# Four graph layers on one core: mask pieces pinned to unit steps, mask sums spread over the units, carries copied a step ahead, and first work of the next stage issued while sums end

## The chip, the cores and the metric

The kernel runs on one core of one Trainium2 chip. The metric is the device time of one execution in microseconds. A core has five engines with a queue each: PE (matrix products), DVE (vector operations), ACT (activations and copies), POOL and SP (here mostly queues that issue DMAs, as ACT's queue does too).

## What is computed

A feature matrix `x` (3327 x 512) goes through four graph layers over one 0/1 adjacency matrix `adj` (3327 x 3327, int32). Each layer's output is added to its input and normalised by row:

```
def attention_layer(x, adj, W, a, heads):       # layers 0, 2, 3 (8, 8 and 4 heads)
    Wh = x @ W                                  # per head
    e = leaky_relu(Wh @ a1 [:, None] + Wh @ a2 [None, :], 0.2)
    p = softmax(where(adj > 0, e, -9e15), axis=neighbours)
    return p @ Wh                               # layers 2 and 3: elu of it

def sage_layer(X, A):                           # layer 1
    keep = (A > 0) & (cumsum(A > 0, axis=1) <= 64)
    mean = (keep @ X) / max(keep.sum(1), 1)
    xj = leaky_relu(mean @ W_nb.T + b_nb);  xi = leaky_relu(X @ W_line.T + b_line)
    return xi + where(keep.sum(1) > 0, xj, 0)

x = layernorm(x + layer(x))                     # four times
```

## The kernel before

The 3327 nodes are 26 tiles of 128 rows; 13 tiles are a half (1664 nodes). Everything of size 3327 x 3327 is made on the fly: one byte mask of the adjacency (`mask`, neighbours on the partitions) is kept on chip for all layers. It is made in layer 0 from the int32 matrix in 104 pieces of 128 x 832: `mask_load` brings one piece (`raw`, 416 KB, issued in turn on SP's and ACT's queues), `mask_set` turns it into bytes, on DVE (L521) or on ACT (L519).

An attention layer is done in three parts.

- Projection. For each tile, `project1` transposes `x` (`pt`, L253; copied to `xT` by ACT, L255), and `project2` multiplies it by the weights (`pw`, L264), makes the exponentials `dc` (L265) and the logit columns `fc`, and writes the scaled features `vt` to DRAM (`v`). `prepare` (L292), for one half, makes the exponential columns `rc` and `qc`, transposes `rc` (`pr`, L304), copies it (`rr`, L306) and stores it (`r`), and makes the scale and bias `sc` and `bi`. `cut` (L316) splits `dc` into bf16 pieces (`pc`) for the softmax denominators and places them in `sden` (L336) and `sm` (L341). `mean` (L279) multiplies the summed `x` by the weights and stores one row `ms`.
- Attention. A loop over two halves of the receiving nodes and four units `s` in each; a unit takes two heads in layers 0 and 2 and one head in layer 3. A unit (`unit`, L345) loads the row factors `rb` of its heads over all partitions and then walks over the 26 tiles of neighbours, one step `j` each. Per step and head DVE makes `t` (L396), ACT makes the byte `y` of its sign (L399), and PE adds the product of `t` with the features `vj` to four sums `po` (L405). Every second step PE adds the denominators of two earlier steps to `pd` (L365, `den`): products of `y` with `sden` in every unit, and products of the mask with `sm`, the mask sums, in unit 0 only. Each step also takes one job from a list `background` and one from a list `aside`. At its end a unit copies `po` to `ob` (L419 on ACT, L421 on DVE); transposes of `ob` (`pt`, L427), copies `hb` and stores to DRAM (`hd`) are jobs of the next unit. After a half's last unit `pd` is copied (`db`) and turned into reciprocals (`pe`, L458, and `rec`).
- Finish. `finish` loads two tiles of the result and of the layer's input (`h`, `xr`), divides, adds, and normalises them (`norm_rows`: Sqrt at L154, the normalising activation at L161). It runs inside the next layer's first part.

In layer 0 the first 38 mask pieces are program text of the projection; the other 66 are `aside` jobs, one a step, each step loading a piece and setting the one before it. The counts of neighbours per block of rows (`count_jobs`, L537) are jobs of units 0 and 2 of the first half, behind empty jobs that hold them back; they give `ctd`, the running counts, in DRAM.

Layer 1 (`sage`, L572) first makes the two linear maps of all tiles (`pz`, L612, and `pi`, L615) and then 13 blocks of 256 receiving nodes. For a block, `kept(b, t)` brings the carry (the running count ahead of the tile, `cy`) into a PSUM bank `pk` (copy by ACT, L680), adds the tile's own running count to it (PE, L681), and compares with 64 on DVE (`kt`, L684). PE then forms the sums `acc` of the kept neighbours (L711) for each of the two tiles of a block in three bf16 parts; `output` finishes the tile, and two jobs (layer 2's `project1` and `project2` of the tile) are taken at steps 11 and 17 of the next sum. Layer 3's projection is `third` (L736), which also finishes layer 2; layer 3's own finish is done in its attention by `later` and `final`.

Two things set the order of the work. On PE the order is that of the program text:

```
ctx.enter_context(tc.manual_schedule(engines={mybir.EngineType.PE}))
```

On DVE, ACT, POOL and SP a scheduler sets the order when the kernel is built, by its own estimate of when each instruction's inputs are ready, so that an instruction may move far from its place in the text. `tc.keep_in_program_order(ins)` takes one instruction out of this freedom: it stays behind the instruction of its engine that is just ahead of it in the text. Pools of buffers give the other ties: `at_t` has 6 buffers for `t` in layers 0 and 2, `at_y` 7 or 8 for `y`, `raw` two for the mask pieces of the attention.

## Time and profile before

| what | value |
|---|---|
| median of the runs | 3514.73 us (3510.88, 3514.73, 3521.66) |
| profiled execution, its own time | 3513.41 us |
| its span | 3511.7 us |
| granted PE clock, mean over the span | 0.981 |
| busy: PE, DVE, ACT, POOL | 95%, 77%, 69%, 5% |
| layer 0: projection; attention | 0 to 164; 164 to 990 us |
| layer 1: linear maps; blocks | 990 to 1205; 1205 to 1840 us |
| layer 2: attention | 1844 to 2640 us |
| layer 3: projection; attention and end | 2640 to 2800; 2800 to 3512 us |

A line of instruction groups in the profile has the source line, engine, operation and tiles, the count, then the busy time in us and the mean in ns of one, and the idle time of the engine ahead of them with what ended most of it. A line of a timeline has start and duration in us, and in brackets the idle time ahead of it with what ended it. PE 95% busy does not mean that PE sets the pace everywhere: it is a mean over stages[...].

### The profile page before, as it was taken

The page shows a single profiled execution, that of the slowest core. Times are in us where ns is not written, and L with a number is a line of the kernel's source. Part 1 is how long each engine was busy: PE and PEld are TensorE (multiplying, and loading weights), DVE is VectorE, ACT ScalarE, POOL GpSimd, SP SyncE. Part 2 cuts the span into 40 slices and gives each one's busy share as a digit, 9 for nine tenths or more (in the row PEclk, how much of TensorE's full clock was granted, in tenths as well). Part 3 has the DMA queues.
Part 4 walks back from the last instruction along what each step waited for, and adds up shares of the span by engine and source line. Part 5 has one row for each costly group of instructions (what it writes and reads, how often), then busy time and mean ns, then how long its engine had stood idle before and what let it go on. Part 6 is the DMA issues. An engine that isn't in the chain of part 4 may idle for free.

```text
span 3511.7 us, 48175 instructions
## 1 busy us (share of the span) xinstructions
PE 3340.7 (95%) x18926; PEld 1705.4 (49%) x18926; DVE 2689.9 (77%) x2751; ACT 2440.2 (69%) x2369; POOL 181.1 (5%) x289
## 2 busy tenths in 40 slices
PE   7899999999989999999989999999998899999997
PEld 6644444444444455545544444444446655455553
DVE  5599999999967544344339999999997666668886
ACT  3678988999953343443328999899996655558885
POOL 1000000000000111111110000000001000000000
PEclk9999999999999999999999999999998999999998
DMA  9713311111133422222211111111106411112211
GB/s 360 231 46 119 99 52 38 56 29 47 37 113 126 133 83 66 75 67 70 70 52 41 48 48 46 52 47 42 38 25 211 149 44 44 44 43 91 81 39 48
DMA packets 208454, 276.67 MB, mean 79 GB/s; under 512 B 19321, under 2 KB 140355, under 8 KB 208228
## 3 DMA queue, kind: packets, MB, share of 16 engines
q1 hardware_dynamic: 173622, 157.37, 14.0%
q0 software_dynamic: 22736, 89.80, 8.1%
q10 hardware_dynamic: 11870, 26.42, 2.3%
q8 instruction: 149, 2.44, 0.3%
q14 instruction: 77, 0.63, 0.1%
HBM read 204.92 MB, written 68.60 MB: 78 GB/s over the span
## 4 chain that ended last, share of the span: by engine, by line
PE 59%; issue 26%; DVE 6%; DMA 5%; ACT 3%; POOL 1%; POOLq 0%; SPq 0%; ACTq 0%; DVEq 0%
PE po L405 33%; PE acc L711 9%; PE pw L264 5%; PE pd L365 4%; DVE t L396 3%; PE pz L612 2%; PE pi L615 2%; DMA raw<-in_adjT_dram 1%; DMA cy<-ctd 1%; ACT y L399 1%; PE pt L427 1%; PE pk L681 1%; DVE kt L684 1%; DMA v<-vt 1%; PE pt L253 1%
## 5 line engine op out<-in xcount | busy, mean ns | idle before, releaser
L396 DVE SCALAR_TENSOR_TENSOR t<-rb,qc,mask 128x1664 f32<-128x1664 f32 x1040 | 1959.5, 1945 | 205.8 <-PE po L405 159.0
L399 ACT ACTIVATE y<-t,bi,sc 128x1664 fp8e4<-128x1664 f32 x1040 | 1772.2, 1766 | 331.9 <-PE pd L365 312.0
L405 PE MATMUL po<-t,vj 128*64 128x448 f32 (+3 forms) x8320 | 1944.2, 521 | 24.1 <-DVE t L396 22.5
L405 PEld LDWEIGHTS po<-t,vj 128*64 128x64 f32 (+1 forms) x8320 | 857.8, 148 | 984.7 <-issue 677.3
L711 PE MATMUL acc<-zs,kt 128*128 128x512 bf16 x1352 | 402.8, 380 | 0.0
L264 PE MATMUL pw<-wsb,xT 128*128 128x264 f32 (+1 forms) x1248 | 303.1, 398 | 21.7 <-DVE vt L270 9.9
L680 ACT CAST pk<-cy 128x256 f32<-128x256 bf16 x338 | 123.9, 374 | 270.5 <-DVE kt L684 218.6
L711 PEld LDWEIGHTS <-kt 128*128 128x128 fp8e4 x2028 | 198.3, 98 | 227.5 <-issue 32.0
L264 PEld LDWEIGHTS pw<-wsb,xT 128*128 128x128 f32 x1248 | 241.3, 198 | 66.6 <-ACT xT L255 13.3
L365 PE MATMUL pd<-y,sden 128*32 128x448 fp8e4 (+1 forms) x4160 | 259.9, 341 | 8.4 <-ACT y L399 8.2
L684 DVE SCALAR_TENSOR_TENSOR kt<-pk,mask 128x256 fp8e4<-128x256 f32 x338 | 140.9, 421 | 158.2 <-PE pk L681 157.6
L711 PE MATMUL acc<-zl,kt 128*128 128x512 bf16 x676 | 256.6, 380 | 0.6 <-DMA zl<-zd 0.6
L365 PEld LDWEIGHTS <-sden 128*32 128x32 bf16 x4160 | 118.0, 96 | 160.3 <-issue 137.7
L270 DVE TENSOR_TENSOR vt<-pw,dc 128x256 f32<-128x256 f32 x156 | 59.0, 417 | 98.7 <-ACT dc L265 86.8
L681 PE MATMUL pk<-mask,upto 128*128 128x256 fp8e4 x338 | 92.2, 273 | 20.4 <-ACT pk L680 19.7
L353 POOL DMA_DIRECT2D rb<-r x40 | 21.4, 537 | 1674.7 <-DVE t L396 1571.8
L612 PE MATMUL pz<-wn,xT 128*128 128x512 f32 x208 | 97.1, 611 | 6.4 <-ACT xT L606 6.4
L268 ACT COPY fc<-pw 128x8 f32<-128x8 f32 (+1 forms) x156 | 22.9, 165 | 106.0 <-PE pw L264 99.2
L521 DVE TENSOR_SCALAR mask<-raw 128x832 fp8e4<-128x832 int32 (+1 forms) x78 | 45.1, 594 | 63.9 <-DMA raw<-in_adjT_dram 63.6
L615 PE MATMUL pi<-wl,xT 128*128 128x512 f32 x208 | 93.5, 592 | 0.0
L585 POOL DMA_DIRECT2D cy<-ctd x91 | 67.8, 745 | 403.6 <-ACT pk L680 270.3
L692 DVE SCALAR_TENSOR_TENSOR y<-acc,cnt,bnb 128x512 f32<-128x512 f32 x26 | 19.5, 751 | 79.0 <-PE acc L711 79.0
(165 smaller groups left out, 1780.3 us busy)
## 6 DMA issues: line engine op xcount, KB each, us to landing
vj<-v SPq DMA_DIRECT2D x312, 128.0 KB
rb<-r POOLq DMA_DIRECT2D x40, 832.0 KB, 4.6
cy<-ctd POOLq DMA_DIRECT2D x78, 256.0 KB, 3.9
v<-vt SPq DMA_DIRECT2D x75, 256.0 KB
h<-hd SPq DMA_DIRECT2D x65, 256.0 KB
raw<-in_adjT_dram ACTq DMA_DIRECT2D x38, 416.0 KB
raw<-in_adjT_dram SPq DMA_DIRECT2D x37, 416.0 KB
hd<-hb SPq DMA_DIRECT2D x60, 256.0 KB
```

The costliest lines, as they stand in the source:

```text
L264: nc.tensor.matmul(pw[e][:, :FW + H], xT[:, c, :], wsb[:, c, e, :], start=c == 0, stop=c == FC - 1)
L365: nc.tensor.matmul(pd[c][32 * kk:32 * kk + 32, :w_], lhsT, rhs, start=(kk, c) not in seen, skip_group_check=final is not None, stop=last a ...
L396: nc.vector.scalar_tensor_tensor(t, rb[k], self.qc[:, j, h:h + 1], mask[:, j, i0:i0 + IW], op0=ALU.max, op1=ALU.mult)
L399: nc.scalar.activation(y, t, AF.Sigmoid, bias=self.bi[:, j, h:h + 1], scale=self.sc[:, j, h:h + 1], saturate=False)
L405: nc.tensor.matmul(po[c][k * D:(k + 1) * D, :z - a_], vj[:, j % 2, k * D:(k + 1) * D], ts[k][:, a_:z], start=j == 0, stop=j == NT - 1)
L585: nc.gpsimd.dma_start(out=cy[:, :n, :], in_=ctd[t:t + n, b * GW:(b + 1) * GW] .rearrange("(o t) i -> o t i", o=1).to_broadcast([P, n, GW]))
L612: nc.tensor.matmul(pz, xT[:, c, :], wn[:, c, :], start=c == 0, stop=c == FC - 1)
L615: nc.tensor.matmul(pi, xT[:, c, :], wl[:, c, :], start=c == 0, stop=c == FC - 1)
L680: nc.scalar.copy(pk, carry[b, t // 4 * 4][:, t % 4, :])
L681: nc.tensor.matmul(pk, upto, mask[:, t, i0:i0 + GW], start=False, stop=True, skip_group_check=True)
L684: nc.vector.scalar_tensor_tensor(kt, pk, NEIGHBOURS, mask[:, t, i0:i0 + GW], op0=ALU.is_le, op1=ALU.mult, saturate=False)
L711: nc.tensor.matmul(acc, kts[t][:, s * P:(s + 1) * P], zs[:, t, c, :] if c < 2 else zl[:, t, :], start=t == 0 and c == 0, stop=t == NT - 1 ...
```

## The change

- Masks. All 104 pieces are one list. The first 60 belong to the projection (three steps of the list at two tiles of five, two at the others), all on DVE; the other 44 are the `aside` jobs of the first two units, and the instruction that sets a piece is pinned to its place in the program text, behind its step's `t` (DVE) or `y` (ACT). The empty jobs ahead of the counts are gone.
- Mask sums. In layers 0 and 2 the mask products of steps `j0` and `j0 + 1` are made in unit `j0 // 2 % 4` instead of all in unit 0.
- Carry. `kept` issues the copy of the next tile's carry into the other `pk` bank right after its own product, instead of its own copy ahead of it.
- Layer 1's last sum. The job at step 17 of the very last sum (layer 2's `project2` of the tile before the last) is left for after the sum.
- `prepare(1)` and `cut(1)`, the parts for the second half of the tiles, become jobs of unit 0 in all three attention layers.
- The pool of `rb` is opened ahead of those of `t`, `y` and `vj`, so that it lies at another place in memory.
- A function `ending` is called in the last unit of layers 0 and 2 ahead of its last `den`: it issues the finish of the layer's first two tiles there, instead of after the attention.

The diff:

```diff
-        def cut(self, pool, half):
+        def cut(self, pool, half, tag="pc", bufs=1):
...
-            pc = pool.tile([P, HALF, H, 8], BF, name="pc")
+            pc = pool.tile([P, HALF, H, 8], BF, name="pc", tag=tag, bufs=bufs)
             nc.gpsimd.memset(pc, 0.0)
-            rest = pool.tile([P, HALF, H], F32, name="rest")
+            rest = pool.tile([P, HALF, H], F32, name="rest", bufs=1)
...
-        def unit(self, pools, half, s, background, aside, final=None):
+        def unit(self, pools, half, s, background, aside, final=None, ending=None):
...
-                if s == 0:
+                if s == (j0 // 2 % NS if HS == 2 else 0):
                     for j, c, k, e in order:
                         a_, w_ = part(c, e)
                         go(c, j0 + j, k, e, self.sm[:, j0 + j, 32 * k:32 * k + 32],
...
+            if ending:
+                ending()
             den(NT - 2, late)
...
-            with tc.tile_pool(name="at_t", bufs=3 * self.HS, reuse_waits="tile") as tp, \
+            with tc.tile_pool(name="at_r", bufs=self.HS + 1, reuse_waits="tile") as rp, \
+                    tc.tile_pool(name="at_t", bufs=3 * self.HS, reuse_waits="tile") as tp, \
                     tc.tile_pool(name="at_y", bufs=4 * self.HS - (self.li == 0), reuse_waits="tile") as yp, \
                     tc.tile_pool(name="at_v", bufs=4, reuse_waits="tile") as vp, \
-                    tc.tile_pool(name="at_r", bufs=self.HS + 1, reuse_waits="tile") as rp, \
...
-                mask_set(held[k - lag], *pieces[k - lag], on_act=(k - lag) in on_act)
+                ins = mask_set(held[k - lag], *pieces[k - lag], on_act=(k - lag) in on_act)
+                if pinned:
+                    tc.keep_in_program_order(ins)
...
+                order = [(b, t) for b in range(len(blocks)) for t in range(NT)]
+                at = [0]
+
+                def carry_in(k):
+                    if k < len(order):
+                        b, t = order[k]
+                        if t % 4 == 0 and groups:
+                            load_carry()
+                        nc.scalar.copy(pks[k % 2], carry[b, t // 4 * 4][:, t % 4, :])
+
                 def kept(b, t):
-                    t0, i0 = blocks[b]
-                    if t % 4 == 0 and groups:
-                        load_carry()
-                    pk = pks[t % 2]
-                    nc.scalar.copy(pk, carry[b, t // 4 * 4][:, t % 4, :])
+                    k = at[0]
+                    at[0] += 1
+                    assert order[k] == (b, t)
+                    i0 = blocks[b][1]
+                    pk = pks[k % 2]
                     nc.tensor.matmul(pk, upto, mask[:, t, i0:i0 + GW], start=False, stop=True,
                                      skip_group_check=True)
+                    carry_in(k + 1)
                     kt = kp.tile([P, GW], F8, name="kt")
...
-                            if jobs and t in (11, 17):
+
+                            if jobs and (t == 11 or t == 17 and not (last and s == G - 1)):
                                 jobs.pop(0)()
...
                 L3.project2(pp, bank, wsb, *pend)
-                L3.prepare(pp, 1)
                 L3.mean(pp, bank, wsb)
-                L3.cut(pp, 1)
...
-                L3.attention(later=later, final=final)
+                L3.attention(lambda pool, half, s: [lambda: L3.prepare(fp, 1, "xr", 2), lambda: L3.cut(fp, 1, "e", 2)]
+                             if (half, s) == (0, 0) else [], later=later, final=final)
...
-            EARLY = 3 * NT // 4
-            msteps = mask_steps(rw0, [(t, q) for t in range(EARLY) for q in range(2)], 3, ())
+            pieces = [(t, q) for t in range(NT) for q in range(2)] + [(t, q) for q in (2, 3) for t in range(NT)]
+            EARLY = 2 * NT + 8
+            msteps = mask_steps(rw0, pieces[:EARLY], 3, (), False)
...
-                for _ in range(2):
+                for _ in range(3 if t % 5 < 2 else 2):
                     if msteps:
                         msteps.pop(0)()
...
-            L0.prepare(pp, 1)
             L0.mean(pp, bank, wsb)
-            L0.cut(pp, 1)
...
-                return [lambda: None] * (2 * (NT - EARLY) + 1) + count_jobs(pool, 0)
+                return [lambda: L0.prepare(f0, 1, "xr", 1), lambda: L0.cut(f0, 1, "h", 2)] + count_jobs(pool, 0)
             if (half, s) == (0, 2):
-                return [lambda: None] * 6 + count_jobs(pool, 1)
+                return count_jobs(pool, 1)
...
-        L0.attention(first_jobs, mask_steps(rawp, pieces, 1, [k for k in range(len(pieces)) if k % 5 in (1, 3)]))
+        pieces = pieces[EARLY:]
+        ends = []
+        L0.attention(first_jobs, mask_steps(rawp, pieces, 1, [k for k in range(len(pieces)) if k % 5 in (1, 3)], True),
+                     ending=lambda: ends.extend(finish(f0, x, L0, 0, 2, 2)))
...
-        sage(finish(f0, x, L0, 0, 2, 2), fin0, x, L0, L2, w2, x2)
-        with tc.tile_pool(name="p", bufs=2, reuse_waits="tile") as pp:
-            L2.prepare(pp, 1)
+        sage(ends, fin0, x, L0, L2, w2, x2)
...
-                with tc.tile_pool(name="p", bufs=2, reuse_waits="tile") as pp:
-                    L2.cut(pp, 0)
-                    L2.cut(pp, 1)
-                L2.attention()
-            third(finish(f2, x2, L2, 0, 2, 2))
+                L2.cut(mp, 0, "pc", 1)
+                L2.attention(lambda pool, half, s: [lambda: L2.prepare(mp, 1, "rr", 1), lambda: L2.cut(mp, 1, "pc", 1)]
+                             if (half, s) == (0, 0) else [],
+                             ending=lambda: ends.extend(finish(f2, x2, L2, 0, 2, 2)))
+            third(ends)
```

More of the change, by code (lines that the diff above doesn't have):

```diff
@@ L471, in unit, with attention @@
             return jobs[:2] + [reciprocals] + jobs[2:]
-        def attention(self, extra=None, aside=(), later=None, final=None):
-            with tc.tile_pool(name="at_t", bufs=3 * self.HS, reuse_waits="tile") as tp, \
+        def attention(self, extra=None, aside=(), later=None, final=None, ending=None):
+            with tc.tile_pool(name="at_r", bufs=self.HS + 1, reuse_waits="tile") as rp, \
+                    tc.tile_pool(name="at_t", bufs=3 * self.HS, reuse_waits="tile") as tp, \
                     tc.tile_pool(name="at_y", bufs=4 * self.HS - (self.li == 0), reuse_waits="tile") as yp, \
                     tc.tile_pool(name="at_v", bufs=4, reuse_waits="tile") as vp, \
-                    tc.tile_pool(name="at_r", bufs=self.HS + 1, reuse_waits="tile") as rp, \
                     tc.tile_pool(name="at_s", bufs=2, reuse_waits="tile") as sp, \
@@ L490, in attention @@
                             aside += later(s)
-                        jobs += self.unit(pools, half, s, jobs, aside, final if half else None)
+                        jobs += self.unit(pools, half, s, jobs, aside, final if half else None,
+                                          ending if (half, s) == (1, NS - 1) else None)
                 while jobs:
@@ L517, in mask_set, with mask_steps @@
         if on_act:
-            nc.scalar.activation(dst, raw[:n, :w_], AF.Sigmoid, bias=below0[:n], scale=400.0, saturate=False)
-        else:
-            nc.vector.tensor_scalar(dst, raw[:n, :w_], 0.0, None, op0=ALU.is_gt, saturate=False)
-    def mask_steps(pool, pieces, lag, on_act):
+            return nc.scalar.activation(dst, raw[:n, :w_], AF.Sigmoid, bias=below0[:n], scale=400.0, saturate=False)
+        return nc.vector.tensor_scalar(dst, raw[:n, :w_], 0.0, None, op0=ALU.is_gt, saturate=False)
+    def mask_steps(pool, pieces, lag, on_act, pinned):
         held = []
@@ L697, in output @@
                     return y
+                carry_in(0)
                 kts = [kept(0, t) for t in range(4)]
@@ L949, in first_jobs @@
             return []
-        pieces = [(t, q) for t in range(EARLY, NT) for q in range(2)] + \
-            [(t, q) for q in (2, 3) for t in range(NT)]
-        L0.attention(first_jobs, mask_steps(rawp, pieces, 1, [k for k in range(len(pieces)) if k % 5 in (1, 3)]))
+        pieces = pieces[EARLY:]
+        ends = []
+        L0.attention(first_jobs, mask_steps(rawp, pieces, 1, [k for k in range(len(pieces)) if k % 5 in (1, 3)], True),
+                     ending=lambda: ends.extend(finish(f0, x, L0, 0, 2, 2)))
     with tc.tile_pool(name="col2", bufs=1) as cp:
@@ L958 @@
         L2.more_columns(cp)
-        sage(finish(f0, x, L0, 0, 2, 2), fin0, x, L0, L2, w2, x2)
-        with tc.tile_pool(name="p", bufs=2, reuse_waits="tile") as pp:
-            L2.prepare(pp, 1)
+        sage(ends, fin0, x, L0, L2, w2, x2)
         with tc.tile_pool(name="fin2", bufs=1) as f2:
-            with tc.tile_pool(name="more2", bufs=1) as mp:
+            ends = []
+            with tc.tile_pool(name="more2", bufs=1, reuse_waits="tile") as mp:
                 L2.piece_columns(mp)
-                with tc.tile_pool(name="p", bufs=2, reuse_waits="tile") as pp:
-                    L2.cut(pp, 0)
-                    L2.cut(pp, 1)
-                L2.attention()
-            third(finish(f2, x2, L2, 0, 2, 2))
+                L2.cut(mp, 0, "pc", 1)
[3 more added lines that the diff above has]
+            third(ends)
 def _layout(inputs):
```

## The prediction

> **What bounds the kernel now.** I read the page's totals and its chain first, then a table of windows cut at each attention unit, then the waits and the timelines of the places where one stage hands over to the next.
>
> ```profile
> PE 3340.7 (95%) x18926; PEld 1705.4 (49%) x18926; DVE 2689.9 (77%) x2751; ACT 2440.2 (69%) x2369; POOL 181.1 (5%) x289
> ...
> PE 59%; issue 26%; DVE 6%; DMA 5%; ACT 3%; POOL 1%; POOLq 0%; SPq 0%; ACTq 0%; DVEq 0%
> ...
> L396 DVE SCALAR_TENSOR_TENSOR t<-rb,qc,mask 128x1664 f32<-128x1664 f32 x1040 | 1959.5, 1945 | 205.8 <-PE po L405 159.0
> ```
>
> The page's `y` row (L399 on ACT) has 1766 ns for one. PE is 95% busy overall and carries 59% of the chain, but that average hides two regimes. In the windows of layer 0's first four units (columns: window, then busy us and count of PE, PEld, DVE, ACT, POOL, clock, DMA share, GB/s) DVE is as full as PE:
>
> ```profile
> 162.20:270.10 107.90, 101.98 (x860) 48.35 (x861) 105.48 (x70) 86.09 (x53) 0.54 (x1) 0.95 0.21 60
> ...
> 488.50:586.30 97.80, 96.70 (x637) 41.12 (x637) 97.44 (x54) 89.97 (x60) 1.06 (x2) 1.00 0.14 44
> ```
>
> The second row shown, unit 3, is a clean unit: 52 `t` instructions start 1.862 us apart (96.9 us). The first three units hold 11 to 19 DVE instructions beyond the 52 (masks, counts, copies) and take 107.9, 111.7 and 106.7 us. So in layers 0 and 2 a DVE instruction put into or taken out of the `t` stream counts in full. In layer 1 and layer 3 PE sets the pace. The rest is in the handovers, where one tile's chain runs alone.
>
> **Projection and start of layer 0.** The same table in stretches of 20 us shows the projection DMA-bound to about 120 us (its last two figures: the DMA engines' share, 1.02, and 372 GB/s); then PE sets the pace at 4.0 us a tile. The PE and DVE timelines show its end, a chain:
>
> ```profile
> 60.00:80.00 20.00, 16.85 (x77) 13.97 (x76) 11.06 (x23) 6.94 (x19) 0.00 (x0) 0.91 1.02 372
> ```
> ```profile
> 150.90 1.04 PE L304 MATMUL pr<-ident,rc 128*8 128x128 f32 x8 [1.89 <-ACT rc L299]
> 153.66 1.23 PE L304 MATMUL pr<-ident,rc 128*8 128x128 f32 x5 [1.73 <-ACT rr L306]
> 154.69 5.80 PE L286 MATMUL pw<-wsb,xm 128*128 128x256 f32 x16
> 164.22 1.01 PE L405 MATMUL po<-t,vj 128*64 128x448 f32 x1 [3.73 <-DVE t L396]
> ```
> ```profile
> 161.71 0.59 DVE L521 TENSOR_SCALAR mask<-raw 128x832 fp8e4<-128x832 int32 x1 [4.70 <-DMA raw<-in_adjT_dram]
> 162.22 5.67 DVE L396 SCALAR_TENSOR_TENSOR t<-rb,qc,mask 128x1664 f32<-128x1664 f32 x3
> ```
>
> The reader sees that the first `t` (162.22) stands behind a mask whose load was 4.70 us late: that load's issue stood on ACT's queue behind the `ms` copies of the mean. In the order of the changed kernel's instructions 61 masks, all on DVE, stand ahead of the first `t` (before: 59 on DVE and 13 on ACT), only one of them after the last tile; 63 raw loads are issued ahead of tile 18's `x` (before about 54); and the transposes of `prepare(1)` stand behind the first `po`. Data ahead of tile 18: 63 x 0.426 MB, 19 tiles of `x` and 17 of `v` at 0.262 MB, 2.1 MB of weights = 38.4 MB, at the row's 372 GB/s 103 us. Then PE needs about 43 us for what is left (ten tiles at 4.0 and the fill), so the last `pw` ends near 146, where now it is 149.0. DVE's own work after it (`rc`, `sc`, `bi`, the cut) takes from 149.0 to 157.0, less two masks of 0.59: first `t` near 153.5, a gain of **8.7 us**. A rule speaks against this move: the Trainium skill, "DMA: Bandwidth & Descriptors", section "Where 436 GB/s comes from", puts the limit between HBM and one core at about 358 GB/s. The row shows 372 for 20 us, over that limit. By 358, tile 18 comes at 107.3 and the gain is 4.4; I keep the row. Bounds: 3 (every added load in the way) to 13.
>
> **Masks in the units.** 43 pieces are left, one a step: 24 in unit 0 (14 on DVE, 10 on ACT), 19 in unit 1 (11 and 8). Unit 0: 96.9 + 14 x 0.59 + counts (four quads at about 1.5) = 111.2, and 1.5 for waits: 112.7. Unit 1: 96.9 + 11 x 0.59 + 3 of copies = 106.4. Unit 2: 96.9 + 6 of counts + 1 = 104. Sum with a clean fourth 420.9, where now it is 424.1: **3.2** gained (bounds: 8 gained to 5 lost). A pinned mask has behind it on DVE the next `t`, and behind that `y`, `po` and `pd`. Its load is issued when the piece two before it is set, so it has about two steps (7.4 us) where the issue is on SP, less where ACT's queue lags behind DVE. The nearest measured wait is small: in 160 to 500 us DVE waited for raw loads 7.7 us in 4 waits, ACT 16.4 in 5. ACT has room: 52 x 1.766 + 10 x 0.99 = 102 of 112. SP's queue has the `vj` loads and the `ctd` and `mask<-nb` stores among the raw loads.
>
> **Mask sums over four units.** The same 416 small matmuls per half, moved from unit 0 to units 0 to 3. In half 1's unit 0 DVE is 101.0 of 103.9 and its extra is copies and reciprocals, not PE; in the other units PE has 0.5 to 1.5 us spare, and the sums add 0.66 a pair to 6.66 for only every fourth pair (DVE needs 7.45). I take **0**, hidden under `t`; bounds 3 gained (layer 0's unit 0) to 3 lost.
>
> **Carry copied a step ahead.** Bounded by this view of layer 1's second part (1260 to 1800 us):
>
> ```profile
> ACT pk L680 <- DVE kt L684: 202.4, 167, 5.8
> ...
> PE pk L681 <- ACT pk L680: 12.7, 14, 1.2
> ```
>
> The copy already runs as soon as `kt` frees its bank, and the order of these copies on ACT is the same in both kernels. PE waited for it 12.7 us in 540. I take **0**; bounds 0 to 11 gained. Not below 0 by itself: no instruction is added.
>
> **Finish of the first tiles while the sums end.** The scheduler had already drawn this work into half 1; its 6 to 7 DVE instructions leave the `t` stream: layer 0 **2.3**, layer 2 about **2** gained net. But on ACT it now stands at the very end:
>
> ```profile
> 990.23 1.78 ACT L399 ACTIVATE y<-t,bi,sc 128x1664 fp8e4<-128x1664 f32 x1
> 991.91 0.46 ACT L419 COPY ob<-po 128x384 f32<-128x384 f32 x1
> 992.51 0.95 ACT L450 COPY db<-pd 64x448 f32<-64x448 f32 x2
> ```
>
> In the order of the changed kernel, ahead of the first line here (the last `y`), come a table load, Sqrt and a table load back (1.28 + 0.29 + 1.28), and between `y` and `db` two normalisations (1.6): the last `pd`, `db` and `pe` come **4.5** later. A second rule bears here: "ScalarE: Activation LUTs", section "What ACT_TABLE_LOAD costs", adds a drain of about 1.38 us to each load of 1.283. In this trace a load at 138.58 is followed by its activation at 139.88, so no drain shows; by the rule the loss is 7.3. I keep the trace. At layer 2's end one Exp with its table load stands before `ob`: **1.7** lost.
>
> **Start of layer 2.**
>
> ```profile
> 1819.14 0.38 PE L711 MATMUL acc<-zl,kt 128*128 128x512 bf16 x1
> 1825.92 1.12 PE L253 MATMUL pt<-ident,y 128*128 128x128 f32 x4 [6.40 <-ACT y L161]
> ```
> ```profile
> 1844.14 1.95 DVE L396 SCALAR_TENSOR_TENSOR t<-rb,qc,mask 128x1664 f32<-128x1664 f32 x1 [2.76 <-DMA rb<-r]
> ```
>
> Tile 24's `project2` (3.7 us of PE) moves from ahead of the last sum into the gap of 6.40: 3.7 gained. The table load before `rc` is gone (1.3). `rb` now lies where `zs` was and is loaded when the last sum ends, so the wait of 2.76 goes, and two of the `sden` and `sm` copies go behind the first `t`s. DVE's cut is late next: last `pw` near 1829, then 6 us of DVE: first `t` near 1835.6, **8.5** gained (bounds 4 to 10).
>
> **Start of layer 3.** Between its last `pw` (2786.4) and its first `po` (2800.11) lie waits of 4.58 for `rc` and 1.82 for `rr`, with 13 transposes and the mean. The waits go, the transposes are paid later: **5** gained (3 to 9).
>
> Sum: 8.7 + 3.2 + 2.3 + 2 + 8.5 + 5 - 4.5 - 1.7 = 23.5. Against the profiled execution's own 3513.4 (span 3511.7 and 1.7 around it) that is 3489.9; the median of the runs shown stands 1.3 above it, so 3491.
>
> **Rivals.** (1) Slower: the pinned masks starve. Place: DVE in units 0 and 1 of layer 0. Each of 25 sets waits w for a load whose issue is stuck behind ACT's `y`s, and holds all `t`s. It decides from w = 23.5/25 = 0.94 us (no gain) and is slower by the bound from 1.4. At 2 us it gives 3491 + 50 = 3541. For it: the 5.8 and 4.7 us longest waits of ACT and DVE for raw. Against: the lag of two steps, and t's six buffers. (2) The projection stays DMA-bound to its end; the start's gain goes: 3500. For: share 1.02 now, nine more loads (9 x 1.15 = 10 us). Against: share falls to 0.76 after 120 us. (3) The handovers cost more (drains, late `h` loads at the third projection, whose PE already idles 14 us), half of the rest is lost: 3504. (4) The carry does bite, 8 of the 11 us: 3483. That parts do nothing (sums, carry) is in the forecast.
>
> **How the numbers follow.** Forecast 0.60 (own range 3477 to 3504), (1) 0.08, (2) 0.16, (3) 0.09, (4) 0.07. A measurement of this kernel can tell about 0.3%, 10.5 us: faster is below 3504.2. Faster: 0.60 + 0.14 + 0.05 + 0.07 = 0.86; same 0.02 + 0.04 + 0.02 = 0.08; slower 0.06, all from (1). The range 3470 to 3509 leaves out most of (1) and the tails.
>
> **What would show it.** Right: first `t` of layer 0 near 153 with one mask row after the last `pw`; 25 DVE and 18 ACT mask rows in units 0 and 1, DVE's wait for raw under 15 us; `acc` of layer 1 at 46 us a block as now; 16 `pw` matmuls inside the 6.4 us gap; first `t` of layer 2 some 8 us sooner after the last `acc`; last `y` of layer 0 followed by `db` 1.6 us later than now. Wrong: units 0 or 1 above 118 us, a last `pw` after 149, or a block of layer 1 under 45 us.

## The result, and the profile after

The changed kernel takes 3493.8 us (median of 3489.1, 3494.2, 3493.7 and 3494.0), the kernel before 3516.5 in the same comparison (3510.9 to 3521.7): a ratio of 0.9933, with a 95% interval of 0.9915 to 0.9951. The prediction's 3491 for 3514.7 is also 0.993. The profiled execution took 3489.1 with a span of 3486.7, 25.0 us under that of before. But the sum came out right over stages that did not: the start and first half of layer 0 together gained nothing, and layer 3's projection gained 14 us that the forecast did not have.

This table was read off the traces: each stretch from one named instruction to the next, in us. Layer 2's eight units with the same instructions take 787 to 796 us from kernel to kernel, so a difference under some 4 us in a long stretch of one profile is read only where the same stretch of the other kernels below agrees with it. That is so for the halves of layer 0: half 1 takes 397.0 to 397.8 us in all ten kernels with the sums spread and 400.3 to 400.9 in the four others; half 0 takes 426.8 to 428.8 in the changed kernel and in all its versions but one (f1), and 424.2 to 426.1 in the kernel before and in the two versions of it without spread sums.

| stretch | before | changed | difference | forecast |
|---|---|---|---|---|
| start to first `t` of layer 0 | 162.2 | 160.8 | -1.4 | -8.7 |
| half 0 of layer 0 | 424.2 | 428.0 | +3.8 | -3.2 |
| half 1 of layer 0, to its last `t` | 400.3 | 397.2 | -3.1 | -2.3 |
| last `t` to first `pz` of layer 1 | 22.4 | 22.9 | +0.5 | +4.5 |
| first `pz` to last output of layer 1 | 810.6 | 809.3 | -1.3 | } -8.5 |
| last output to first `t` of layer 2 | 24.6 | 19.4 | -5.2 | } |
| units of layer 2 | 792.5 | 790.5 | -2.0 | -2.0 |
| layer 3's projection: last `t` to last `pw` | 149.8 | 135.7 | -14.1 | +1.7 |
| last `pw` to first `t` of the next unit | 91.6 | 89.0 | -2.6 | -5.0 |
| the rest | 633.7 | 634.0 | +0.3 | 0 |

The page's totals and chain (before: 3340.7 and 59%): PE is as full as it was, of a shorter span.

```profile
PE 3325.6 (95%) x18873; PEld 1701.2 (49%) x18926; DVE 2694.9 (77%) x2759; ACT 2396.6 (69%) x2336; POOL 181.2 (5%) x289
...
PE 62%; issue 24%; DVE 6%; DMA 5%; ACT 3%; POOL 1%; POOLq 0%; DVEq 0%; SPq 0%; ACTq 0%
```

**Layer 0's start.** The projection's first five windows, the timelines of PE, POOL and DVE (the `rb` load of before went out at 103.17):

```profile
0.00:20.00 20.00, 7.85 (x36) 7.57 (x37) 7.48 (x11) 1.87 (x2) 12.66 (x26) 1.00 0.92 340
20.00:40.00 20.00, 18.92 (x86) 15.71 (x85) 11.28 (x22) 3.06 (x13) 0.00 (x0) 1.00 0.99 345
40.00:60.00 20.00, 12.71 (x60) 10.38 (x60) 11.00 (x22) 2.38 (x12) 0.00 (x0) 1.00 0.99 341
60.00:80.00 20.00, 15.18 (x65) 12.44 (x66) 12.39 (x26) 2.64 (x13) 0.00 (x0) 0.91 1.02 379
80.00:100.00 20.00, 16.23 (x71) 13.25 (x70) 12.53 (x28) 3.76 (x17) 0.00 (x0) 0.91 1.02 347
```
```profile
95.26 5.49 PE L264 MATMUL pw<-wsb,xT 128*128 128x264 f32 x16 [1.95 <-DVE vt L270]
...
102.87 3.73 PE L264 MATMUL pw<-wsb,xT 128*128 128x264 f32 x16
...
143.76 7.29 PE L264 MATMUL pw<-wsb,xT 128*128 128x264 f32 x32
150.88 3.62 PE L286 MATMUL pw<-wsb,xm 128*128 128x256 f32 x16
162.76 1.76 PE L405 MATMUL po<-t,vj 128*64 128x448 f32 x2 [8.27 <-DVE t L396]
```
```profile
155.98 1.84 POOL L353 DMA_DIRECT2D rb<-r  x3 [23.43 <-DVE pc L329]
```
```profile
157.66 0.58 DVE L524 TENSOR_SCALAR mask<-raw 128x832 fp8e4<-128x832 int32 x1
160.75 1.95 DVE L396 SCALAR_TENSOR_TENSOR t<-rb,qc,mask 128x1664 f32<-128x1664 f32 x1 [2.51 <-DMA rb<-r]
```

Counted back from the last two tiles at 143.76, the `pw` at 102.87 is tile 14's, so twelve tiles were left when the mask loads were done (DVE's last wait for one ended at 103.03), and PE ran them with one stop of 0.66 us, at 4.0 us each, to 151.05. The transposes are gone from ahead of the first `po`, as the prediction said, and one mask stands after the last `pw`. The first `t` then waits for `rb`: its pool now lies where the columns are that `cut(1)` reads, so POOL could issue the load only at 155.98.

**Half 0.** The first two units and the last of the half in the table of windows (before: 107.9, 111.7 and 97.8 us), unit 1 of the kernel before, DVE's wait for mask loads in 158 to 500 us, and one place in unit 0 on PE, ACT and DVE:

```profile
160.80:275.80 115.00, 105.19 (x756) 44.07 (x758) 110.26 (x78) 94.08 (x64) 1.06 (x2) 0.96 0.39 118
275.80:385.20 109.40, 103.09 (x749) 50.47 (x747) 103.79 (x68) 94.40 (x66) 1.07 (x2) 0.97 0.44 131
...
490.60:588.80 98.20, 96.88 (x673) 43.64 (x670) 97.52 (x55) 91.23 (x61) 1.06 (x2) 1.00 0.14 44
```
```profile
270.10:381.80 111.70, 105.01 (x739) 48.87 (x735) 102.78 (x65) 94.08 (x65) 1.60 (x3) 0.98 0.36 112
```
```profile
DVE mask L524 <- DMA raw<-in_adjT_dram: 1.2, 2, 0.6
```
```profile
176.12 0.27 PE L304 MATMUL pr<-ident,rc 128*8 128x128 f32 x1 [3.21 <-ACT rr L306]
176.32 5.81 PE L405 MATMUL po<-t,vj 128*64 128x448 f32 x32
```
```profile
171.68 0.57 ACT L306 COPY rr<-pr 8x512 f32<-8x512 f32 x1 [2.67 <-PE pr L304]
```
```profile
179.44 5.68 DVE L396 SCALAR_TENSOR_TENSOR t<-rb,qc,mask 128x1664 f32<-128x1664 f32 x3 [2.92 <-ACT y L399]
```

The pinned masks hardly wait: 1.2 us on DVE and none on ACT, where DVE waited 7.7 (4.7 of them ahead of the first `t`) and ACT 16.4 before. But the moved `prepare(1)` now stands between two steps of `po`. ACT, whose copies `rr` stand among the `y`, stands 2.67 us for the first transposes; PE's last transpose waits 3.21 us for ACT's second copy, which runs only behind two `y`; and DVE stands 2.92 us until a `y` is done. Unit 1 has no such place, but DVE is busy for only 103.79 of its 109.40 us (before: 102.78 of 111.70).

**Layer 0 to layer 1, layer 1, layer 2's start.**

```profile
989.64 1.28 ACT L154 ACT_TABLE_LOAD   x1
990.93 0.29 ACT L154 ACTIVATE rs<-mv,eps 128x2 f32<-128x2 f32 x1
991.25 1.28 ACT L399 ACT_TABLE_LOAD   x1
992.54 1.77 ACT L399 ACTIVATE y<-t,bi,sc 128x1664 fp8e4<-128x1664 f32 x1
994.22 1.50 ACT L161 ACTIVATE h<-h,rs 128x512 f32<-128x512 f32 x2
```
```profile
1817.87 3.72 PE L264 MATMUL pw<-wsb,xT 128*128 128x264 f32 x16
1823.96 0.66 PE L253 MATMUL pt<-ident,y 128*128 128x128 f32 x4 [2.37 <-ACT fc L268]
```

ACT's line stands as predicted, and without a drain after the table loads (the Sqrt starts 1.29 us after the first load starts), so the 4.5 of the trace and not the rule's 7.3 was the right size up to `pe`. `pe` starts 11.2 us after the last `t`, where that was 7.1. At the handover ACT's copy `hb` waits for the store of an earlier one, before and changed, and POOL's first load for layer 1 (the last `t` ended at 986.64 and at 985.91):

```profile
1007.54 0.91 ACT L433 COPY hb<-pt 128x512 f32<-128x512 f32 x2 [6.91 <-DMA hd<-hb]
992.30 0.76 POOL L585 DMA_DIRECT2D cy<-ctd  x1 [105.18 <-ACT y L399]
```
```profile
1006.83 0.58 ACT L435 COPY hb<-pt 128x512 f32<-128x512 f32 x1 [1.23 <-DMA hd<-hb]
985.89 0.76 POOL L590 DMA_DIRECT2D cy<-ctd  x1 [99.00 <-ACT y L399]
```

In layer 1 the next to last tile's `pw` fills the gap behind the last sum. A pair of sums takes 46.0 us (24.1 and 21.9 between outputs) in both kernels, and PE's wait for the carry's copies is 12.4 us for 12.7.

**Layer 3's projection.** SP's queue just after layer 2's last `t` (before, then changed), and PE's first stall (before: 6.13 us for `h`):

```profile
2643.86 1.03 SPq L133 DMA_DIRECT2D x<-h  x2
2650.07 0.37 SPq L436 DMA_DIRECT2D hd<-hb  x1
2650.49 0.98 SPq L126 DMA_DIRECT2D h<-hd  x2
2652.49 2.16 SPq L436 DMA_DIRECT2D hd<-hb  x2
2654.70 0.50 SPq L126 DMA_DIRECT2D h<-hd  x1
```
```profile
2630.53 2.71 SPq L126 DMA_DIRECT2D h<-hd  x6
```
```profile
2652.81 1.12 PE L253 MATMUL pt<-ident,h 128*128 128x128 f32 x4 [2.76 <-ACT h L161]
```

Last `t` ended at 2636.6 before and at 2628.0 after. Six `h` loads (tiles 2 and up, whose rows were stored long ago) go out by 5 us after it in the changed kernel; before, three of them stood behind stores of the last unit, up to 18 us after it. One row for the stretch from first to last `pw`, before and changed:

```profile
2654.80:2786.40 131.60, 111.50 (x525) 93.15 (x525) 102.88 (x243) 89.73 (x192) 13.09 (x25) 0.94 0.60 198
```
```profile
2646.30:2763.70 117.40, 108.38 (x526) 92.13 (x527) 96.80 (x236) 88.39 (x191) 12.57 (x24) 0.97 0.67 220
```

The same products: PE idles 9.0 us instead of 20.1, and with fewer long pauses its granted clock is 0.97 instead of 0.94 and its busy time 3.1 us shorter.

### The profile page after: what moved, and what is told of

The parts are those of the page before. It is cut to its first block, busy times and chain, and to the rows that moved or that the text cites. A ratio compares the mean times of both kernels' runs of the same rounds, so it can differ in the third digit from the quotient of the medians.

```text
span 3486.7 us, 48120 instructions
## 1 busy us (share of the span) xinstructions
PE 3325.6 (95%) x18873; PEld 1701.2 (49%) x18926; DVE 2694.9 (77%) x2759; ACT 2396.6 (69%) x2336; POOL 181.2 (5%) x289
## 3 DMA queue, kind: packets, MB, share of 16 engines
q1 hardware_dynamic: 173622, 157.37, 14.1%
## 4 chain that ended last, share of the span: by engine, by line
PE 62%; issue 24%; DVE 6%; DMA 5%; ACT 3%; POOL 1%; POOLq 0%; DVEq 0%; SPq 0%; ACTq 0%
PE po L405 34%; PE acc L728 9%; PE pw L264 5%; PE pd L365 5%; DVE t L396 3%; PE pz L617 2%; PE pi L620 2%; DMA raw<-in_adjT_dram 2%; ACT y L399 1%; DMA cy<-ctd 1%; PE pt L429 1%; PE pk L696 1%; PE pt L253 1%; DVE kt L700 1%; PE pe L460 1%
## 5 line engine op out<-in xcount | busy, mean ns | idle before, releaser
L405 PE MATMUL po<-t,vj 128*64 128x448 f32 (+3 forms) x8320 | 1939.5, 522 | 26.0 <-DVE t L396 24.6
L264 PE MATMUL pw<-wsb,xT 128*128 128x264 f32 (+1 forms) x1248 | 299.3, 395 | 21.7 <-DVE vt L270 19.5
L264 PEld LDWEIGHTS pw<-wsb,xT 128*128 128x128 f32 x1248 | 238.9, 196 | 65.6 <-issue 18.8
L365 PE MATMUL pd<-y,sden 128*32 128x448 fp8e4 (+1 forms) x4160 | 259.8, 342 | 10.5 <-ACT y L399 10.5
L700 DVE SCALAR_TENSOR_TENSOR kt<-pk,mask 128x256 fp8e4<-128x256 f32 x338 | 140.9, 421 | 159.5 <-PE pk L696 158.9
L365 PEld LDWEIGHTS <-sden 128*32 128x32 bf16 x4160 | 117.8, 96 | 162.4 <-issue 139.8
L708 DVE SCALAR_TENSOR_TENSOR y<-acc,cnt,bnb 128x512 f32<-128x512 f32 x26 | 19.5, 751 | 85.1 <-PE acc L728 85.1
L524 DVE TENSOR_SCALAR mask<-raw 128x832 fp8e4<-128x832 int32 (+2 forms) x86 | 50.2, 592 | 45.0 <-DMA raw<-in_adjT_dram 44.4
```

Of the source, the lines that this page charges most:

```text
L264: nc.tensor.matmul(pw[e][:, :FW + H], xT[:, c, :], wsb[:, c, e, :], start=c == 0, stop=c == FC - 1)
L365: nc.tensor.matmul(pd[c][32 * kk:32 * kk + 32, :w_], lhsT, rhs, start=(kk, c) not in seen, skip_group_check=final is not None, stop=last a ...
L405: nc.tensor.matmul(po[c][k * D:(k + 1) * D, :z - a_], vj[:, j % 2, k * D:(k + 1) * D], ts[k][:, a_:z], start=j == 0, stop=j == NT - 1)
L700: nc.vector.scalar_tensor_tensor(kt, pk, NEIGHBOURS, mask[:, t, i0:i0 + GW], op0=ALU.is_le, op1=ALU.mult, saturate=False)
```

## The experiments

Times are medians, with the ratio to the kernel before and its interval from the same comparison (the median of before is 3520 to 3522 in them, so ratios are compared, not times). The stretches are those of the table above.

| kernel | ratio (95%) | first `t` | half 0 | half 1 | last `t` to `pz` | layer 2's start | layer 3's projection | next unit |
|---|---|---|---|---|---|---|---|---|
| changed | 0.9933 (0.9915 to 0.9951) | 160.8 | 428.0 | 397.2 | 22.9 | 19.4 | 135.7 | 89.0 |
| e1, no `ending` in layer 2 | 0.9943 (0.9923 to 0.9962) | 161.8 | 428.2 | 397.8 | 22.9 | 20.0 | 139.1 | 88.9 |
| e2, no `ending` in layer 0 | 0.9930 (0.9911 to 0.9949) | 162.0 | 427.9 | 397.2 | 22.2 | 18.8 | 141.2 | 87.4 |
| e3, masks as before | 0.9936 (0.9919 to 0.9952) | 162.9 | 428.8 | 397.3 | 22.9 | 19.8 | 139.9 | 87.4 |
| e4, `rb` of layer 0 as before | 0.9930 (0.9912 to 0.9948) | 158.9 | 426.8 | 397.5 | 25.9 | 20.1 | 138.2 | 89.1 |
| e5, `prepare(1)`, `cut(1)` as before | 0.9933 (0.9918 to 0.9948) | 162.0 | 427.3 | 397.1 | 22.9 | 20.7 | 139.8 | 94.5 |
| e6, `project2` and carry as before | 0.9935 (0.9921 to 0.9950) | 162.2 | 428.4 | 397.1 | 22.9 | 21.2 | 135.5 | 89.1 |
| e8, sums in unit 0 | 0.9933 (0.9916 to 0.9949) | 160.3 | 428.6 | 400.9 | 18.6 | 20.0 | 141.0 | 89.4 |
| before + spread sums | 0.9964 (0.9951 to 0.9977) | 163.5 | 418.9 | 397.4 | 26.1 | 24.9 | 151.0 | 92.7 |
| before + `rb` pool first | 1.0010 (1.0003 to 1.0016) | 177.8 | 425.4 | 400.3 | 19.0 | 27.6 | 143.9 | 95.7 |
| before + layer 2's jobs | 0.9989 (0.9983 to 0.9996) | 163.0 | 426.1 | 400.3 | 22.4 | 24.9 | 146.7 | 93.1 |
| before + sums + layer 2's jobs | 0.9976 (0.9968 to 0.9984) | 161.5 | 419.3 | 397.0 | 25.8 | 25.5 | 145.0 | 92.3 |
| f1, changed, layer 0's front as before | 0.9904 (0.9890 to 0.9917) | 161.7 | 420.4 | 397.8 | 25.6 | 19.5 | 138.8 | 89.0 |

### Where layer 3's projection gained

e1:

```diff
-                             ending=lambda: ends.extend(finish(f2, x2, L2, 0, 2, 2)))
-            third(ends)
+                             ending=None)
+            third(finish(f2, x2, L2, 0, 2, 2))
```

> The changed kernel, with the finish of layer 2's first two tiles issued after the attention again (layer 2's `ending` left out). In the changed kernel layer 3's projection takes 135.7 us from the last `t` of layer 2 to the last `pw`, before it took 149.8. Theory A: the 14 us come from `ending` in layer 2, because the finish of tiles 0 and 1 no longer stands among the first ones of the projection and the Exp and Sqrt table loads fall otherwise. Then this kernel has 146 to 151 us in that stretch and is 10 to 15 us slower than the changed kernel. Rival B: they come from the other place of the pools or from the moved `prepare(1)` and `cut(1)` of layer 3. Then the stretch stays at 134 to 139 us and the time within 4 us. In either case last `t` to `pe` is about 1.5 us shorter (8.2 in the changed kernel, 6.7 before) and half 1 of layer 2 about 2 us longer.

139.1 us: theory A fell. The stretch is 135.5 to 141.2 in the changed kernel and in every version of it with one part undone, also where that part lies in layer 0 alone (e2 to e4: 138.2 to 141.2). So the changed kernel's 135.7 is at the low end, the gain is 9 to 14 us, and differences of 5 us between two profiles are scatter or order here. `pe` came 7.4 us after the last `t` (8.2), and layer 2's units took 794.7 us in all for 790.5, inside the scatter named above.

e8: `if s == 0:` instead of `if s == (j0 // 2 % NS if HS == 2 else 0):`.

> The changed kernel with the mask sums all in unit 0 again, all else as changed. The PE products are the same. In the kernel's order of instructions only this edit, of all parts undone one by one, changes the order of DVE and ACT in layer 3's projection by much. Theory A: the 10 to 14 us that layer 3's projection gained (last `t` of layer 2 to last `pw`: 149.8 before, 135.7 to 141.2 in the changed kernel and four variants of it) come from that other order, which the scheduler chose because the sums put work into layer 2's last unit; undone, the stretch takes 145 to 152 us and the kernel is 8 to 14 us slower than the changed one. Rival B: the order differs but the stretch stays at 134 to 142 us, and the gain belongs to what is left (the finish's buffers, the moved cut). Theory and rival both expect the units of layers 0 and 2 unchanged within 2 us each (DVE sets their pace), except unit 0 of layer 0, where PE is busiest: up to 3 us longer.

141.0 us: A fell again. Both theories missed what the edit did do: half 1 of layer 0 is 3.7 us longer (its first two units 104.4 and 100.1 for 103.1 and 98.0) and the handover after it 4.3 shorter. With the sums in unit 0 the scheduler draws the finish of tiles 0 and 1 into half 1 (its last activation ends some 79 us ahead of the last `t`, as before); with spread sums the work stands at the half's end, with `ending` or without. `pe` starts 7.1 us after the last `t` here and before, 11.2 in the changed kernel, 10.5 in e2 without `ending`.

The sums alone, on the kernel before:

> The kernel before, with only the mask sums spread over the four units. Theory A: layer 3's projection becomes shorter from this alone, 134 to 142 us for 149.8 from last `t` to last `pw`, and the kernel is 8 to 14 us faster than before; the attention units keep their lengths within 1 us except unit 0 of layer 0 (107.9), 1 to 3 us shorter. Rival B: the stretch stays at 145 to 152 us: the order that pays comes only with other parts, and this kernel is within 4 us of before.

151.0 us in the projection, so rival B's mechanism there; but the kernel is 10 us faster than before. Half 0 (418.9 for 424.2, with units 0 and 1 at 102.8 and 109.2 for 107.9 and 111.7) and half 1 gain 8 us, and the handover gives 3.7 back (26.1 for 22.4). The two profiles differ by 3.3 us in all, so the traces do not show where the rest of the 10 lies.

The `rb` pool first, on the kernel before, and layer 2's `prepare(1)` and `cut(1)` as jobs, on the kernel before:

> The kernel before, with only the pool of `rb` opened first in the attention. Theory A: the gain in layer 3's projection belongs to the order of DVE and ACT that the scheduler finds there. This edit alone moves that order away from the one of before, and close to that of the changed kernel with the sums in unit 0, which ran 141.0 us. So: last `t` of layer 2 to last `pw` 137 to 143 us (149.8 before, 151.0 with the sums alone). Rival B: the order is not the cause, or the place of the pools alone matters otherwise: 147 to 152 us. Layer 2's start: `rb` goes out when the last sum of layer 1 ends, so the wait of 2.76 us for it goes; 21 to 23 us from the last output of layer 1 to the first `t` (24.6 before, 19.4 in the changed kernel). Layer 0: `rb` waits for `cut(1)`, the first `t` 0 to 3 us later than before. Time 8 to 14 us faster than before by A, 0 to 4 by B.

> The kernel before, with only layer 2's `prepare(1)` and `cut(1)` as jobs of unit 0. No pool of layer 3's projection moves, but the order of DVE and ACT in that projection is the same as with the `rb` pool moved (99% of the instructions in line). Theory A (the order is the cause): last `t` of layer 2 to last `pw` is 137 to 143 us here too, within 3 us of the kernel with the `rb` pool moved. Rival C (the place of the pools is the cause): 147 to 152 us here, and 137 to 143 only there. Layer 2's start 1 to 4 us shorter than 24.6, its units within 2 us of 792.5.

143.9 and 146.7 us: neither gains all, both lie near the border of A and its rivals, and the 3 us of the second are within the scatter of this stretch. The `rb` pool alone makes the kernel slower. In layer 2 the prediction's wait for `rb` becomes longer, not shorter, because without the moved cut `rb` lies over what the cut reads; in layer 0 the two masks ahead of the first `t` wait for their loads. POOL and DVE of this kernel:

```profile
1858.29 1.58 POOL L353 DMA_DIRECT2D rb<-r  x3 [15.38 <-DVE sm L341]
```
```profile
1863.95 7.73 DVE L396 SCALAR_TENSOR_TENSOR t<-rb,qc,mask 128x1664 f32<-128x1664 f32 x4 [6.21 <-DMA rb<-r]
```
```profile
177.34 0.59 DVE L521 TENSOR_SCALAR mask<-raw 128x832 fp8e4<-128x832 int32 x1 [8.17 <-DMA raw<-in_adjT_dram]
```

The two edits that give nearly the changed kernel's order, together:

> The kernel before, with the spread mask sums and layer 2's `prepare(1)` and `cut(1)` as jobs of unit 0 together; the text of layer 3's projection and its pools are as before. Alone, the first of these left that projection at 151.0 us and the second brought it to 146.7 (149.8 before). Together they give an order of DVE and ACT in it that is 94% and 95% in line with that of the changed kernel (before: 55% and 46%). Theory A: the order is the cause, and the order of the changed kernel comes only from the two together: 135 to 142 us, and the time 12 to 18 us under before (the sums alone were 10 to 12 under). Rival B: the two add up singly: 147 to 150 us; then something else in the changed kernel (the `rb` pool, `ending`, the moved `prepare(1)` of layer 3) is needed.

145.0 us: between A and B once more. An order 94% alike does not give the time. Its first stall is shorter than before's 6.13, but one `pw` late in the stretch waits 4.25 us where the changed kernel waits 0.79. What is settled: the gain is in stalls of PE and the clock that follows them, it needs no edit of the projection's text, no single part carries it, and of the parts tried alone only the `rb` pool (6 us) moved it by more than the scatter, and by little. What stays open: how much of the rest is order, and how much the place of buffers that the `rb` pool moves as well.

### Layer 0's start and first half

e3: `EARLY` 38, two steps a tile, `pinned` false, the empty jobs back.

> The changed kernel with the mask part undone: 38 pieces in the projection and 66 in the units, not pinned, counts behind the empty jobs again; all else as changed. Theory A: the mask part as it stands gained nothing: nine more loads ahead of the last tiles moved the projection's end from 149.0 to 151.1, and the pinned sets and earlier counts made half 0 428.0 for 424.1. Undone, the last `pw` ends near 149, the first `t` comes near 157 to 159 (no transposes ahead of it), half 0 takes 422 to 426, and the kernel is 4 to 8 us better than the changed one. Rival B: the old masks on ACT would again put table loads and late loads ahead of the first `t`; first `t` near 161, half 0 near 424 to 428, and the time the same within 3 us. Rival C: the pins help, half 0 is above 430 without them and the time is 5 us or more worse.

Rival B, nearly: the last `pw` at 149.8 (151.0), first `t` 162.9, half 0 428.8. The mask part by itself is worth nothing that can be told, either way.

e4: the pool `at_r` is opened behind `at_v` where `self.li == 0`.

> The changed kernel with the pool of `rb` at its old place in layer 0 only (behind the pools of `t`, `y` and `vj`). Theory A: in the changed kernel `rb` of layer 0 lies over the columns that `cut(1)` reads, so that POOL issued its load at 156.0 after DVE's `pc` (before: at 103.2), and the first `t` waited 2.51 us for it and the third 0.69. At its old place the load goes out near 105, the first `t` stands right behind the last mask at 158 to 159 (160.8 now), and the time is 2 to 3 us better. Rival B: another buffer now lies over these columns (`t` itself), and the first `t` waits for `cut(1)` on the same engine at no cost, so that still gives the gain; but if the wait goes to `y` or `vj`, the first `po` stays at 162.8 and the gain is under 1 us.

As A for its place: the first `t` at 158.9, 1.9 us sooner, with the last `pw` 0.8 later. The handover after layer 0 took 3.0 us more (PE waits 3.98 us ahead of the first `pz`, 1.22 in the changed kernel), so the time did not show it. The same place set first on the kernel before, in the run of the `rb` pool alone, took the handover from 22.4 to 19.0: there it gains, by the wait for the store of `hb` (2.90 us for 6.91 in that run; 4.75 here).

e5: `prepare(1)` and `cut(1)` back in the text of all three projections.

> The changed kernel with `prepare(1)` and `cut(1)` back ahead of the first `po` in all three attention layers. Theory A: in layer 0 the move gains 3 us ahead of the first `t` and gives them back in unit 0, where PE waits 3.2 us for an `rr` buffer between two groups of transposes, `po` comes late, and DVE stands 2.9 us for a `t` buffer. Undone: last `pw` to first `t` 12 to 14 us (9.8 in the changed kernel), unit 0 of layer 0 111 to 113 us (115.1); layer 2's start 1 to 3 us later, layer 3's last `pw` to second unit 91 to 92 us (89.0). Sum: 2 to 5 us slower than the changed kernel. Rival B: unit 0 stays at 115, the wait was not its cause; then 5 to 9 us slower.

A holds in direction: 11.2 us from last `pw` to first `t` (9.8), unit 0 113.5 (115.1), layer 2's start 1.3 later, layer 3's 5.5 later. In layer 0 the move is worth nothing net (half 0 is 427.3 for 428.0); it pays in layer 3. The whole time does not tell 3 us. The wait of 3.2 us in unit 0 is for ACT's copy, as the lines above show, and not for a buffer `rr`.

f1: the masks of e3, the `rb` place of e4 and layer 0's `prepare(1)` and `cut(1)` ahead of the attention, together; all else as changed.

> The changed kernel with three parts taken back in layer 0 only: the masks (38 pieces in the projection, not pinned, empty jobs ahead of the counts), the place of the `rb` pool, and `prepare(1)` and `cut(1)` ahead of the attention. Spread sums, `ending`, layer 1, 2 and 3 as changed. In order, DVE and ACT of the first half of layer 0 are those of the kernel with the sums spread alone, which came to the start of half 1 at 582.4 us, where the changed kernel came at 588.8. Theory A: the parts that touch layer 0's start and first half lose 6 us together, hidden in the total by the gains of layers 2 and 3; without them the start of half 1 is at 581 to 584 us and the kernel 4 to 8 us faster than the changed one, median near 3488 where that was 3494. Rival B: the parts are worth nothing either way and 582.4 was the scatter of one run: 586 to 589 us, and the time within 3 us of the changed kernel.

A: half 1 starts at 582.2 us (588.8 in the changed kernel), and the median is 3488.3, with a ratio of 0.9904 for 0.9933: the fastest version here. Its interval and the changed kernel's touch (0.9917 and 0.9915). Of the 6.6 us it gives 2.7 back at the handover, where the `rb` pool's old place costs what it cost in e4. Undone one at a time, the same parts gave half 0 at most 1.2 us (426.8 to 428.8); undone together, 7.6. Which of them hinder each other was not tested. The table of windows of its first and third unit, after the row of unit 0 shown above:

```profile
161.70:264.60 102.90, 99.68 (x734) 44.48 (x734) 102.90 (x66) 84.57 (x51) 0.53 (x1) 0.97 0.10 30
...
374.50:484.30 109.80, 106.63 (x793) 50.77 (x793) 108.20 (x76) 95.13 (x66) 1.06 (x2) 1.00 0.34 96
```

DVE is busy in all of unit 0 (102.90 of 102.90; 110.26 of 115.00 in the changed kernel): no late `po`, no late `rb`, and the masks have gone to units 1 and 2, where the scheduler found them room.

### The handover and layer 1

e2: `ending=None` in layer 0, and `finish` back in the call of `sage`.

> The changed kernel, with layer 0's `ending` left out (the finish of tiles 0 and 1 is issued after the attention). Theory A (the reading of the two traces): the last `db` comes some 3.5 us earlier again, but PE then waits some 6 us for `xT` ahead of the first `pz`, as before, so last `t` to first `pz` is 22 to 24 us as in both kernels; the 6 to 7 DVE instructions go back into half 1 of layer 0, which becomes about 3 us longer (400 for 397). Sum: 2 to 4 us slower than the changed kernel. Rival B (the prediction's step): the 4.5 us of the handover are real, then last `t` to first `pz` is 18 to 19 us and the time 1 to 3 us better than the changed kernel.

22.2 us from last `t` to first `pz`: A for the handover, and B fell. But half 1 stayed at 397.2 and `pe` came only 0.7 us sooner, so `ending` is not what took the finish out of the `t` stream and put it at the end.

e6: `carry_in(k)` ahead of the product instead of `carry_in(k + 1)` behind it, and `t in (11, 17)`.

> The changed kernel with two parts of layer 1 undone, which the trace tells apart: the carry copied in its own step again, and layer 2's `project2` of the last tile but one back inside the last sum. Theory A for the carry: a pair of sums takes 46.0 us in both kernels and still does here. Rival: the copy a step ahead pays and the pairs become 46.2 to 46.9 us. For `project2`: the last sum takes 20.8 us again for 17.3, and from its end to the first `t` of layer 2 19 to 20 us (19.4 in the changed kernel), so the end of layer 1 to the first `t` comes 2 to 4 us later in all. Sum: 2 to 4 us slower than the changed kernel; with the rival for the carry 5 to 14.

The pairs of sums take 46.0 us here too: the carry part is worth nothing. The last sum takes 20.8 us (17.3), layer 2's start 21.2 (19.4): deferring `project2` is worth 5 us by the traces, more than expected. The whole time (0.9935) has too wide an interval to confirm it.

## Why the prediction was right, and where not

- **Start of layer 0, 8.7 forecast, 1.4 measured.** The step that failed is the 103 us at which tile 18's data were to be there; the 43 us behind it held. Tile 18's load went out at 107.35, and the last `pw` ended 43.7 us later, at 151.05 (a last `pw` after 149 was one of the prediction's own signs of being wrong). The 103 came from one window's 372 GB/s. The five windows shown above reach 379 once and have a mean of 350, the same windows of before 348. The Trainium skill's "DMA: Bandwidth & Descriptors" (section "Where 436 GB/s comes from") gives about 358, and by it the prediction had 107.3 us and a gain of 4.4; e4, where the first `t` does not wait for `rb`, gained 3.3. So the page's figure sized this sum better than the one row did, although single rows are above it; that 107.3 and 107.35 are so close is luck, for tile 18's load waited for one of the three buffers of `x`, which tile 15's transposes left at 107.04. What held the projection back to 103 us was DVE: its masks waited 31.7 us for their loads between 20 and 103 us, and `vt`, for which PE waited 1.95 us at 95.26, stood behind one of them. How much of that is the rate and how much the order of the loads stays open. The other 2.5 us are a wait that the sum did not have: `rb` behind `cut(1)`, because of the pool's new place. The prediction used the new place for layer 2 and did not ask what lies there in layer 0. This is the second rival's outcome, but not its mechanism: the DMA engines' share was down to 0.65 in 100 to 120 us and 0.39 in 120 to 140.
- **Masks and half 0, 3.2 gained forecast, 3.8 lost.** The pins behaved (1.2 us of waits; the first rival, slower by starved masks, is out). Units 0 to 2 took 115.1, 109.3 and 105.4 us where the sum had 112.7, 106.4 and 104. In unit 0 the missing term is the stall of 2.92 us at the moved `prepare(1)`, whose transposes the prediction let be "paid later" only in layer 3. In unit 1 the sum had no term for waits, where DVE stood 8.9 us before and stands 5.6 now. This reads the trace; undoing the masks (e3), the place of `rb` (e4) or `prepare(1)` (e5) singly did not give half 0 back, undoing the three together (f1) did.
- **Sums, forecast 0.** On the changed kernel, undoing them moves the ratio by nothing (give or take 0.0025, 9 us); alone on the kernel before they gain 10 us. They move the scheduler's finish work out of half 1 (3 us, which the prediction booked under `ending`) and give DVE a unit 0 without stalls if nothing else fills it.
- **`ending`, 4.5 lost and 2.3 and 2 gained.** The loss was of the right size, with another cause and a gain beside it that the prediction did not have. `pe` came 4.1 us later, as the order said, and the handover with it: 3.7 us longer with the sums spread on the kernel before (26.1 for 22.4), 4.3 on the changed one (22.9 for e8's 18.6). By e2 and e8 the cause is the spread sums, not `ending`. Only 0.5 was left because the new place of `rb` in layer 0 takes 3.0 to 3.4 us off the same handover (e4; the `rb` pool alone). In all eight kernels with the new place POOL's first loads for layer 1 go out with the last `t` and ACT's longest wait for the store of `hb` is 0.56 to 2.90 us; in the six with the old place they go out 5.7 to 9.1 us behind it and the wait is 4.45 to 7.77. That the later loads stand in that store's way is likely, but not shown.
- **Carry 0.** Right, by the trace and e6.
- **Layer 2's start, 8.5 forecast, 6.5 measured** (5.2 and 1.3; the last sum of layer 1 by itself is 3.5 shorter, which makes 8.7, and the rest of that stretch is within scatter): the gap was filled, `rb` waited for nothing, DVE's cut set the end, as said.
- **Layer 3's projection, 1.7 lost forecast, 14.1 gained.** `pe` was 1.5 us later (8.2 for 6.7), as said; the forecast stopped there and took the rest of the projection as unchanged, though the order of DVE and ACT in it had changed by half. Of the 20.1 us of idle PE there 11.1 went, and 3.1 us of busy time with them. This is luck in the sum: no step of the prediction saw it, and the runs bound its causes without settling them.
- **Layer 3's start, 5 forecast, 2.6 measured;** e5 puts it at 5.5.

Put together, layer 0 up to its last `t` was 13.5 us too hopeful and the stages behind it (layer 1, layer 2's and layer 3's start) about 4; the handover was 4 us too careful and layer 3's projection 16. The range held for the wrong reason as much as for the right ones.

## What to carry to other kernels

Where a scheduler sets the order, list the stretches whose order changes, not only the lines that the edit touches, and put a range on each: here the largest gain came in a projection whose text was edited only behind its last product. When a pool moves, ask at every use of it what lay there and who reads that last. A part undone from the whole and the same part alone on the old kernel can give different answers (the sums: nothing and 10 us, a difference just clear of the noise), and so can single parts and the same parts together (half 0: at most 1.2 us each, 7.6 together), so both are needed before a part is credited.

## What was not expected of the hardware

A group of 16 fp32 products of the first projection takes 3.73 us unbroken. Behind a pause of PE it takes either 3.80 to 3.83 us, at a granted clock of 1.00, or 5.3 us and more, at 0.71 or less. The length of the pause alone does not decide which. In the changed kernel:

```profile
42.58 3.80 PE L264 MATMUL pw<-wsb,xT 128*128 128x264 f32 x16 [2.75 <-DVE vt L270]
60.69 5.49 PE L264 MATMUL pw<-wsb,xT 128*128 128x264 f32 x16 [2.11 <-DVE vt L270]
```

Over the fourteen traces of this case, none of the 64 pauses of 0.3 to 1.82 us in that projection slowed the group behind it, all 11 of 3.05 us and more did, and of the 38 between 1.88 and 2.95 us 22 did. So a pause of some 2 us can cost nearly as much again in the work behind it. In layer 3's projection, from the first `pw` to the last, PE had six pauses of 2 us and more before (6.13, 2.83, 2.74, 3.48, 2.05 and 2.01) and has two now (2.76 and 2.47), and 3.1 us of busy time went with the 11.1 of idle time.
